# Scores by queries and again by keys in the first attention of a two-layer gated kernel

## The chip, the cores and the metric

The kernel runs on one core of a Trainium2 chip. A core has five engines that work side by side: TensorE (PE, with its weight loads listed as PEld), VectorE (DVE), ScalarE (ACT), GpSimd (POOL) and SyncE (SP), which here issues most DMAs. Each runs its own instructions in order and waits for the others by semaphores. The metric is the device time of one execution in microseconds (us), the median of several runs. Lower is better.

## The reference

The input is 16 sequences of 112 tokens of width 256, and for each sequence a context of 375 rows of width 256. Two layers follow one another, each a gated cross-attention and a gated feed-forward with experts. Everything is in 32-bit floats. The change touches only the first attention, which has 16 heads of width 16:

```
xn = layernorm(x)                                  # 16 x 112 x 256
q, k, v = xn@Wq + bq,  ctx@Wk + bk,  ctx@Wv + bv   # per head, 16 wide
w = softmax(q @ k.T / 4)                           # 112 x 375 for each head
x = x + tanh(g_xattn[0]) * ((w @ v).joined @ Wo + bo)
x = x + tanh(g_ffn[0]) * experts0(layernorm(x))    # 14 routed (best 2), 2 shared
x = x + tanh(g_xattn[1]) * attention1(layernorm(x), ctx)
x = x + tanh(g_ffn[1]) * experts1(layernorm(x))
```

The layer norm in front of the first attention has no weights.

## The kernel before

The tokens lie 128 to a tile, 14 tiles (NT). The first attention works on one sequence b at a time, and within it on four quads c of four heads each. That gives 64 quads, and the main loop of the first attention has one step n for each. A head is 16 wide and its slot in the array is 32 rows (HP), so four heads fill the 128 rows. The rows of a slot hold two heads of k; q has zeros in the half of the slot that the quad does not use.

A step before the change has these pieces, in the order in which they are written:

- `scores` (lines 506 to 525) makes q·k for quad n: 4 products with 32 rows each, one for each row group of the array, queries (112) on the partitions of the result and keys (375) along it. VectorE takes the maximum of each row, negated (line 520), and ScalarE makes the exponentials with that maximum as bias (line 522), into `p`.
- `apply` (line 539) multiplies the turned exponentials of quad n - 2 by the values, 12 products (3 chunks of 125 keys, 4 heads), each in one column group of the array. The values carry a column of ones, so the sums of the softmax come with them.
- `turn` (line 527) turns `p` of quad n - 1, so that keys lie on the partitions: 12 transposes on TensorE, and 4 copies out of PSUM, two on VectorE (line 535) and two on ScalarE (line 537).
- Side work, put by hand at a step and at one of three places in it by `at(step, place, f, ...)` and run by `beside`: keys (line 432), values (443) and queries (460) of a coming sequence, the two transposes that bring the result of a sequence into rows of channels (`first_turn`, `second_turn`), the output projection (`project`), the layer norm of the feed-forward behind it (`measured1`, `normed1`, `turned1`) and the logits of its router.

All of this is under `tc.manual_schedule()`: each engine runs its instructions in the order in which they are written. Constants and gates ahead of it (lines 109 to 161) are placed by the planner. In PSUM, `scores` has two slots of two banks, `bank()` three single banks in turn, and the result of `apply` one.

Each product of 32-bit floats is recorded as two weight loads and two matmuls, and each transpose as one of each. So `scores` shows 8 matmuls a step, `apply` 24, `turn` 12.

Ahead of step 0 the program measures and turns the first four token tiles, makes the keys, queries and values of sequence 0 and the scores of quad 0, and turns tiles 4 and 5. After the last quad, eight pieces of the shared experts (`hidden_piece`, `output_piece`) run one to a step, until the logits of the last token tile are made. The shared experts then go on, with the routing beside them, and the routed experts follow.

Of the kernel before, what the change touches and what calls it, by code (L numbers as in the profile page):

```python
# [51 lines left out]
def tile_flamingo(  # L52
# [55 lines left out]

    ident = const.tile([P, P], F32, tag="ident", name="ident")
    make_identity(nc, ident)  # L110

    bits_i = const.tile([P, 1], I32, tag="bits_i", name="bits_i")
    nc.gpsimd.iota(bits_i, pattern=[[0, 1]], base=0, channel_multiplier=1)
    nc.vector.tensor_scalar(bits_i, bits_i, HD, None, ALU.bitwise_and)
    halves = const.tile([P, 2], F32, tag="halves", name="halves")
    nc.vector.tensor_copy(halves[:, 1:2], bits_i)
# [38 lines left out]
    nc.scalar.activation(tg, rows_sb[:, 4 * D : 4 * D + 4], AF.Tanh)  # L155

    rowsg = const.tile([P, 4, D], F32, tag="rowsg", name="rowsg")
    for j, g in enumerate((0, 1, 3, 3)):
        nc.vector.tensor_scalar(
            rowsg[:, j, :], rows_sb[:, j * D : (j + 1) * D], tg[:, g : g + 1], None, ALU.mult  # L160
        )
# [252 lines left out]

    with tc.tile_pool(name="a0", bufs=2) as a0, tc.tile_pool(
        name="a0_s", bufs=2, space=PSUM
    ) as ps_s, tc.tile_pool(name="a0_t", bufs=3, space=PSUM) as ps_t, tc.tile_pool(
        name="a0_o", bufs=1, space=PSUM
    ) as ps_o, tc.manual_schedule():
# [5 lines left out]
        bqs = a0.tile([P, NQ], F32, tag="bqs", name="bqs", bufs=1)  # L425
        G = 4
        kts, qts, xns = {}, {}, {}

        def bank():
            return ps_t.tile([P, 512], F32, tag="t", name="pt")  # L430

        def keys(b, c):
            if c == 0:
                kts[b] = a0.tile([P, KD, S], F32, tag="kt", name="kt")
            pk = bank()[:, :S]
            for k in range(KD):
                nc.tensor.matmul(  # L437
                    pk, wk0_sb[:, k, c * P : (c + 1) * P], ctxs[b][:, k, :],
                    start=(k == 0), stop=(k == KD - 1),
                )  # L440
            nc.vector.tensor_scalar(kts[b][:, c, :], pk, col("bk0", c), None, ALU.add)

        def values(b, s0, n):
            pv = bank()[:SC].rearrange("p (j d) -> p j d", d=D)
            for j in range(n):
                s = s0 + j
                for k in range(KD):
                    nc.tensor.matmul(  # L448
                        pv[:, j, :], ctxs[b][:, k, s * SC : (s + 1) * SC], wv0_sb[:, k, :],
                        start=(k == 0), stop=(k == KD - 1),  # L450
                    )
            for j in range(n):
                to = vas[b % 2][:, s0 + j, :, 0:HD]
                v = pv[:, j, :].rearrange("p (h k) -> p h k", k=HD)
                if n == 1:
                    nc.scalar.copy(to, v)
                else:
                    nc.vector.tensor_copy(to, v)

        def queries(b0, g):  # L460

            if g == 0:
                qts[b0 // G] = a0.tile([P, NQ, G * TQ], F32, tag="qt", name="qt")
            pq = bank()[:, : G * TQ]
            for k in range(KD):
                nc.tensor.matmul(
                    pq, wq0_sb[:, k, g * P : (g + 1) * P],
                    xT[:, k, b0 * TQ : (b0 + G) * TQ],
                    start=(k == 0), stop=(k == KD - 1),
                )  # L470
            for u in range(2):
                c = 2 * g + u
                nc.scalar.activation(  # L473
                    qts[b0 // G][:, c, :], pq, AF.Identity, bias=bqs[:, c : c + 1],
                    scale=halves[:, u : u + 1],
                )
# [29 lines left out]
        def scores(b, c):  # L506
            qt, kt = qts[b // G], kts[b]
            t0 = (b % G) * TQ
            sps = [ps_s.tile([P, 2, 512], F32, tag="s", name="sp") for _ in range(2)]
            for j in range(4):  # L510
# [3 lines left out]
                    qt[r : r + HP, c, t0 : t0 + TQ], kt[r : r + HP, c // 2, :],  # L514
                    start=True, stop=True,
                )
            p = a0.tile([TQ, 4, S], F32, tag="p", name="p")
            for h, sp in enumerate(sps):
                mx = a0.tile([TQ, 2], F32, tag="mx", name="mx", bufs=4)
                nc.vector.tensor_reduce(mx, sp[:TQ, :, :S], AX.X, ALU.max, negate=True)  # L520
                for j in range(2):
                    nc.scalar.activation(  # L522
                        p[:, 2 * h + j, :], sp[:TQ, j, :S], AF.Exp, bias=mx[:, j : j + 1]
                    )
            return p

        def turn(p, pT, j):
            pp = bank()[:SC, : NSC * TQ]
            for s in range(NSC):
                nc.tensor.transpose(  # L530
                    pp[:, s * TQ : (s + 1) * TQ], p[:, j, s * SC : (s + 1) * SC],
                    ident[:TQ, :TQ],
                )
            if j % 2 == 0:
                nc.vector.tensor_copy(pT[:, j, :], pp)  # L535
            else:
                nc.scalar.copy(pT[:, j, :], pp)  # L537

        def apply(b, c, pT, po):
            va = vas[b % 2]  # L540
            for s in range(NSC):
                for j in range(4):
                    r = j * HP
                    nc.tensor.matmul(  # L544
                        po[r : r + HP, c, :], va[:, s, (c // 2) * 8 + j * 2 + c % 2, :],
# [3 lines left out]

        outs = {}  # L550
# [13 lines left out]
        def second_turn(b):  # L564
# [4 lines left out]
            for k in range(KD):  # L569
                nc.vector.tensor_scalar(  # L570
                    oT[:, k, b * TQ : (b + 1) * TQ], pt[:, k, :], col("bv0", k), None, ALU.add
                )
# [31 lines left out]
        def turned1(i):  # L604
# [6 lines left out]
            nc.vector.tensor_copy(xT[:, :, i * P : (i + 1) * P], pt)  # L611
# [14 lines left out]
        def at(step, place, f, *args):  # L626
            side.setdefault((step, place), []).append((f, args))


        hT = hidden_rows()  # L630

        def score_bank():
            return ps_s.tile([P, 2, 512], F32, tag="s", name="pd")[:, 0, :]

        pieces = [(hidden_piece, (score_bank, hT, 0, *blocks[0], m)) for m in range(KH)]
        pieces += [
            (output_piece, (score_bank, hT, 0, blocks[0][0], j)) for j in range(blocks[0][1])
        ]
        for n, (f, args) in enumerate(pieces):
            at(last + n, 0, f, *args)  # L640

        at(8, 2, shared_weights, 0)
        at(10, 2, shared_weights, 1)
        for i in (0, 2, 4):
            at(4 + i // 2, 2, biased, i)

        for i, n in ((6, 1), (8, 5), (10, 0), (12, 4)):
            at(n, 2, measured, i)
            at(n + 2, 2, normed0, i)
            at(n + 3, 1, turned, i)  # L650
            at(n + 3, 2, biased, i)
        for b in range(B):
            n0 = b * NQ
            if b + 2 < B:
                at(n0, 0, context, b + 2)
            if b + 1 < B:
                at(n0, 0, keys, b + 1, 0)
                at(n0 + 1, 0, keys, b + 1, 1)
                at(n0 + 1, 1, values, b + 1, 2, 1)
                at(n0 + 2, 0, values, b + 1, 0, 2)  # L660
# [3 lines left out]
            at(n0 + NQ + 2, 1, first_turn, b)  # L664
            at(n0 + NQ + 3, 0, second_turn, b)
        for i in range(NT):
            n = (((i + 1) * P - 1) // TQ + 2) * NQ
# [4 lines left out]
            at(n + 5, 1, logits, i)  # L672


        nc.vector.tensor_scalar(bqs, col("bq0", 0, NQ), HD**-0.5, None, ALU.mult)
        measured(0)
        measured(2)
        for t in vas:
            nc.gpsimd.memset(t, 0.0)
            nc.gpsimd.memset(t[:, :, :, HD : HD + 1], 1.0)  # L680
        normed0(0)
        turned(0)
        normed0(2)
        turned(2)
        keys(0, 0)
        queries(0, 0)
        ps, pTs = {0: scores(*quads[0])}, {}
        keys(0, 1)
        queries(0, 1)
        values(0, 0, 2)  # L690
        values(0, 2, 1)
        measured(4)
        normed0(4)
        turned(4)
        po = None

        def beside(n, place):
            for f, args in side.get((n, place), ()):
                f(*args)

        for n in range(max(side)[0] + 1):
            if 0 < n < last:
                ps[n] = scores(*quads[n])
            ended = None
            if 0 <= n - 2 < last:
                b, c = quads[n - 2]
                if c == 0:
                    po = ps_o.tile([P, NQ, TQ], F32, tag="av", name="po")
                apply(b, c, pTs.pop(n - 2), po)
                ended = b if c == NQ - 1 else None  # L710
            beside(n, 0)
            turning = 0 <= n - 1 < last
            if turning:
                pTs[n - 1] = a0.tile([SC, 4, NSC * TQ], F32, tag="pT", name="pT")
                for j in range(2):
                    turn(ps[n - 1], pTs[n - 1], j)
            if ended is not None:
                outs[ended] = a0.tile([P, NQ, TQ], F32, tag="oS", name="oS")
                nc.scalar.copy(outs[ended], po)
            beside(n, 1)  # L720
            if turning:
                for j in range(2, 4):
                    turn(ps[n - 1], pTs[n - 1], j)
                ps.pop(n - 1)
            beside(n, 2)

# [534 lines left out]
```

## Time and profile before

| what | before |
|---|---|
| median of 4 runs | 1044.06 us (1041.44 to 1046.28) |
| the profiled execution's own time | 1039.07 us |
| its span, first to last instruction | 1037.4 us |
| mean granted TensorE clock | 0.981 |
| PE busy in the span | 959.6 us (93%), 6474 matmuls |
| DVE busy | 552.5 us (53%) |
| ACT busy | 355.6 us (34%) |
| POOL busy | 184.3 us (18%) |
| 0 to 32.94 us (up to the scores of quad 1) | PE busy 17.5 us, granted clock 0.95 |
| 32.94 to 377.68 us (scores of quad 1 to those of quad 63) | PE 320.3, DVE 237.9, ACT 196.7, POOL 54.7 us busy, clock 1.00 |
| 377.68 to 405.37 us (up to the rest of the shared experts) | PE 25.6 us busy |
| 405.37 to 456.7 us (shared experts, routing) | PE 49.9 us busy |

In the profile, a line "out<-in" names the tile that an instruction writes and those that it reads. The count after "x" is the number of instructions; "busy" is their union, so overlapping ones count once. The idle time of a group is what its engine waited just before it, with the releaser. A matmul's own duration runs from its issue to its modelled end, and several are in flight, so the distance between starts tells more than the duration. In the timeline, each line gives the start and the length of a run of like instructions.

### The profile page before, as it was taken

How to read it: one execution, taken by the hardware profiler on the slowest of the kernel's cores; microseconds unless marked ns; L12 is line 12 of the kernel's file. 1: busy time of each engine (PE TensorE's matmuls, PEld its weight loads, DVE VectorE, ACT ScalarE, POOL GpSimd, SP SyncE). 2: the span in 40 equal slices, each digit the busy share in tenths (PEclk: the TensorE clock that was granted, in tenths of full speed). 3: DMA queues.
4: the chain of work that ended last, by engine and by line, in shares of the span. 5: the costliest groups of instructions: out<-in, count | busy, mean ns of one | idle time of the engine just before them, and what ended most of it. 6: DMA issues, size and time to landing. Idle time of an engine off the chain costs nothing.

```text
span 1037.4 us, 16798 instructions
## 1 busy us (share of the span) xinstructions
PE 959.6 (93%) x6474; PEld 711.1 (69%) x6474; DVE 552.5 (53%) x1352; ACT 355.6 (34%) x757; POOL 184.3 (18%) x323
## 2 busy tenths in 40 slices
PE   5899999999999989999999997899998999999995
PEld 2566666666666656688888883767786676666664
DVE  4676667676667754722222224364444756565675
ACT  2456555555655553101111111114222322222232
POOL 2251111111111112032222206350005000000033
PEclk9999999999999999999999999889998999999998
DMA  6400001001002000429999963234420000000001
GB/s 233 153 2 1 21 21 41 21 21 36 1 21 66 27 6 11 163 72 329 330 319 313 322 230 94 75 120 139 144 75 1 1 21 21 1 1 1 1 30 41
DMA packets 34303, 91.43 MB, mean 88 GB/s; under 512 B 4288, under 2 KB 17984, under 8 KB 28976
## 3 DMA queue, kind: packets, MB, share of 16 engines
q1 hardware_dynamic: 30368, 80.79, 23.1%
q0 software_dynamic: 3312, 9.05, 3.2%
q8 instruction: 51, 0.84, 0.3%
q10 hardware_dynamic: 544, 0.52, 0.1%
q14 instruction: 28, 0.23, 0.1%
HBM read 81.31 MB, written 9.04 MB: 87 GB/s over the span
## 4 chain that ended last, share of the span: by engine, by line
PE 73%; DVE 9%; DMA 7%; ACT 4%; issue 2%; another core or an unknown queue 2%; POOL 0%; SPq 0%; POOLq 0%; DVEq 0%; ACTq 0%
PE ph L1088 9%; PE py L1118 9%; DMA wr_sb<-in_wr_dram 7%; PE sp L512 5%; PE pt L448 5%; PE pt L437 5%; PE phr L763 4%; PE pt L530 4%; PE pyr L775 4%; PE po L544 3%; PE py L403 3%; PE po L998 2%; ACT p L522 2%; PE ph L393 2%
## 5 line engine op out<-in xcount | busy, mean ns | idle before, releaser
L522 ACT ACTIVATE p<-sp,mx 112x375 f32<-112x375 f32 x256 | 125.7, 574 | 96.1 <-DVE mx L520 96.1
L520 DVE TENSOR_REDUCE mx<-sp 112x2 f32<-112x750 f32 x128 | 114.1, 933 | 35.5 <-PE sp L512 32.8
L530 PE MATMUL pt<-ident,p 112*125 112x112 f32 x768 | 110.9, 276 | 16.8 <-DVE oT L570 10.4
L530 PEld LDWEIGHTS pt<-ident,p 112*125 112x125 f32 x768 | 100.4, 188 | 36.1 <-DVE oT L570 12.5
L1088 PE MATMUL ph<-w1b_sb,xT 128*128 128x512 f32 x224 | 102.1, 600 | 0.0
L1118 PE MATMUL py<-w2b_sb,hT 128*128 128x256 f32 x448 | 100.8, 382 | 0.0
L1118 PEld LDWEIGHTS py<-w2b_sb,hT 128*128 128x128 f32 x448 | 82.2, 190 | 14.0 <-ACT hT L1110 4.2
L763 PE MATMUL phr<-xgT,wr_sb 128*128 128x128 f32 x656 | 83.8, 281 | 5.4 <-DVE xgT L753 5.0
L535 DVE COPY pT<-pt 125x336 f32<-125x336 f32 x128 | 64.1, 501 | 42.3 <-PE pt L530 42.2
L763 PEld LDWEIGHTS phr<-xgT,wr_sb 128*128 128x128 f32 x656 | 77.5, 191 | 11.4 <-DVE xgT L753 11.2
L753 DVE TENSOR_SCALAR xgT<-px,wr_sb 128x128 f32<-128x128 f32 x82 | 25.0, 347 | 113.0 <-DMA wr_sb<-in_wr_dram 97.7
L174 POOL TENSOR_SCALAR rstd<-mv 128x1 f32<-128x1 f32 (+2 forms) x23 | 5.2, 224 | 420.2 <-DVE mv L167 420.2
L775 PE MATMUL pyr<-wr_sb,hTr 128*128 128x256 f32 x328 | 77.4, 379 | 0.0
L768 ACT ACTIVATE hTr<-phr 128x512 f32<-128x512 f32 x41 | 24.5, 597 | 152.2 <-PE phr L763 136.1
L537 ACT COPY pT<-pt 125x336 f32<-125x336 f32 x128 | 56.6, 442 | 49.5 <-PE pt L530 48.4
L1088 PEld LDWEIGHTS ph<-w1b_sb,xT 128*128 128x128 f32 x224 | 41.7, 191 | 42.4 <-issue 38.7
L744 POOL DMA_INDIRECT xg_sb<-xn_rows,taker x41 | 39.0, 952 | 155.0 <-PE px L751 115.6
L775 PEld LDWEIGHTS pyr<-wr_sb,hTr 128*128 128x128 f32 x328 | 59.3, 190 | 6.4
L1095 ACT ACTIVATE rh<-mvh,eps 128x1 f32<-128x1 f32 x56 | 16.3, 292 | 131.4 <-DVE mvh L167 131.4
L544 PEld LDWEIGHTS po<-pT,va 125*32 125x32 f32 x1536 | 35.7, 109 | 36.0 <-issue 31.0
L512 PE MATMUL sp<-kt,qt 32*112 32x375 f32 x512 | 57.6, 519 | 0.8 <-ACT qt L473 0.8
L544 PE MATMUL po<-pT,va 125*32 125x112 f32 x1536 | 52.8, 263 | 0.4 <-ACT pT L537 0.4
(231 smaller groups left out, 1466.3 us busy)
## 6 DMA issues: line engine op xcount, KB each, us to landing
wr_sb<-in_wr_dram SPq DMA_DIRECT2D x41, 1025.0 KB
ctx_sb<-in_ctxT_dram SPq DMA_DIRECT2D x32, 375.0 KB
ctxn_sb<-in_ctxN_dram SPq DMA_DIRECT2D x16, 375.0 KB
yg<-yr SPq DMA_DIRECT2D x41, 128.0 KB
w1b_sb<-in_w1b_dram SPq DMA_DIRECT2D x4, 512.0 KB
w2b_sb<-in_w2b_dram SPq DMA_DIRECT2D x4, 512.0 KB
xn_rows<-xn SPq DMA_DIRECT2D x14, 128.0 KB
out_dram<-yf SPq DMA_DIRECT2D x14, 128.0 KB
```

The costliest lines, as they stand in the source:

```text
L437: nc.tensor.matmul(pk, wk0_sb[:, k, c * P : (c + 1) * P], ctxs[b][:, k, :], start=(k == 0), stop=(k == KD - 1),)
L512: nc.tensor.matmul(sps[j // 2][:TQ, j % 2, :S], qt[r : r + HP, c, t0 : t0 + TQ], kt[r : r + HP, c // 2, :], start=True, stop=True,)
L520: nc.vector.tensor_reduce(mx, sp[:TQ, :, :S], AX.X, ALU.max, negate=True)
L522: nc.scalar.activation(p[:, 2 * h + j, :], sp[:TQ, j, :S], AF.Exp, bias=mx[:, j : j + 1])
L530: nc.tensor.transpose(pp[:, s * TQ : (s + 1) * TQ], p[:, j, s * SC : (s + 1) * SC], ident[:TQ, :TQ],)
L535: nc.vector.tensor_copy(pT[:, j, :], pp)
L537: nc.scalar.copy(pT[:, j, :], pp)
L544: nc.tensor.matmul(po[r : r + HP, c, :], va[:, s, (c // 2) * 8 + j * 2 + c % 2, :], pT[:, j, s * TQ : (s + 1) * TQ], start=(s == 0), stop= ...
L763: nc.tensor.matmul(ph[:, m, :], a[:, k, m * P : (m + 1) * P], xgT[:, k, :], start=(k == 0), stop=(k == KD - 1),)
L775: nc.tensor.matmul(py, hT[:, m, :], c[:, m, :], start=(m == 0), stop=(m == KH - 1))
L1088: nc.tensor.matmul(ph, xT[:, k, i * P : (i + 1) * P], a[:, k, :], start=(k == 0), stop=(k == KD - 1),)
L1118: nc.tensor.matmul(py, hT[:, m, j * P : (j + 1) * P], c[:, m, :], start=(m == 0), stop=(m == KH - 1),)
```

## The change

`scores` makes only the maxima. The exponentials are taken from a second product, made by keys. For this, each half of a slot gets its own copy of the keys: in copy u one row of the slot that q leaves at zero is set to one. The negated maximum of each query is put in that same row of q, so the product by keys comes out with the maximum already taken off, and ScalarE makes the exponential without a bias, in the layout that `apply` needs. `turn` is gone. `scores` needs the matching copy of the keys too, and there the row of q is still zero.

The order of a step is now: `scores(n)`, `apply(n - 2)`, side place 0, `maxima(n)`, side place 1, `turned_scores(n)`, side place 2. In PSUM there are two named pairs of banks, for scores and for the side work of places 1 and 2, and four named single banks, for the product by keys, for `apply`, for the turned maxima and for the side work of place 0. Every one has one buffer.

```
+    written = ExitStack()
+    written.enter_context(tc.manual_schedule())      # now from the constants on
...
+    # spots[:,0:2]: one in row 16 (0) of each slot; spots[:,2:4] = 1 - spots[:,0:2]
+    def gated(j):                                     # was at the start
+        if j == 0:
+            nc.scalar.activation(tg, rows_sb[:, 4 * D : 4 * D + 4], AF.Tanh)
+        g = (0, 1, 3, 3)[j]
         nc.vector.tensor_scalar(
             rowsg[:, j, :], rows_sb[:, j * D : (j + 1) * D], tg[:, g : g + 1], None, ALU.mult
         )
...
+        def pair(h):
+            return ps_s.tile([P, 2, 512], F32, tag=f"s{h}", name=f"sp{h}")
+        def single(j):
+            return ps_t.tile([P, 512], F32, tag=f"t{j}", name=f"pt{j}")
         def bank():
+            n, place["n"] = place["n"], place["n"] + 1
+            if place["at"] == 0:
+                return single(1 + n % 2)
+            if n % 2 == 0:
+                place["pair"] = pair(n // 2 % 2)
+            return place["pair"][:, n % 2, :]
...
         def keys(b, c):
-            nc.vector.tensor_scalar(kts[b][:, c, :], pk, col("bk0", c), None, ALU.add)
+            nc.vector.tensor_scalar(
+                kts[b][:, c, 0, :], pk, spots[:, 2:3], bks[:, c, 0:1], ALU.mult, ALU.add
+            )
+            nc.scalar.activation(
+                kts[b][:, c, 1, :], pk, AF.Identity, bias=bks[:, c, 1:2], scale=spots[:, 3:4]
+            )
-        def values(b, s0, n):        # two chunks (DVE copies) or one (ACT copy)
+        def values(b, s):            # one chunk, copied by ACT
...
         def queries(b0, g):          # two outputs: were both ACT, now one DVE, one ACT
...
         def scores(n):
             ...                      # the 4 products as before, on kt[..., u, :]
-            p = a0.tile([TQ, 4, S], F32, tag="p", name="p")
             for h, sp in enumerate(sps):
-                mx = a0.tile([TQ, 2], F32, tag="mx", name="mx", bufs=4)
-                nc.vector.tensor_reduce(mx, sp[:TQ, :, :S], AX.X, ALU.max, negate=True)
-                for j in range(2):
-                    nc.scalar.activation(
-                        p[:, 2 * h + j, :], sp[:TQ, j, :S], AF.Exp, bias=mx[:, j : j + 1]
-                    )
+                nc.vector.tensor_reduce(
+                    mz[:, 2 * h : 2 * h + 2, HD * (1 - u)], sp[:TQ, :, :S], AX.X, ALU.max,
+                    negate=True,
+                )
-        def turn(p, pT, j):          # 3 transposes and a copy; 4 calls a step
+        def maxima(n):
+            pm = single(3)[:, :TQ]
+            nc.tensor.transpose(pm, mzs[c % 2], ident[:TQ, :TQ])
+            qms[n] = a0.tile([P, TQ], F32, tag="qm", name="qm")
+            nc.vector.tensor_tensor(qms[n], pm, qts[b // G][:, c, t0 : t0 + TQ], ALU.add)
+        def turned_scores(n):
+            sts = [single(j) for j in range(4)]
             for s in range(NSC):
                 for j in range(4):
                     r = j * HP
+                    nc.tensor.matmul(
+                        sts[j][:SC, s * TQ : (s + 1) * TQ],
+                        kt[r : r + HP, c // 2, c % 2, s * SC : (s + 1) * SC], qm[r : r + HP, :],
+                        start=True, stop=True,
+                    )
+            pT = a0.tile([SC, 4, NSC * TQ], F32, tag="pT", name="pT")
+            for j in range(4):
+                nc.scalar.activation(pT[:, j, :], sts[j][:SC, : NSC * TQ], AF.Exp)
+            return pT
         def apply(n, pT):            # into single(0), copied by ACT every step
...          # second_turn's result and turned1's: DVE -> ACT
-            at(last + n, 0, f, *args)                 # the eight expert pieces
+            at(last + n, 1, f, *args)
+        for j in range(4):
+            at(1 + j // 2, 2, gated, j)
-        for i, n in ((6, 1), (8, 5), (10, 0), (12, 4)):
+        for i, n in ((4, 3), (6, 7), (8, 15), (10, 19), (12, 23)):
             at(n, 2, measured, i); at(n + 2, 2, normed0, i); at(n + 3, 0, turned, i)
+        at(0, 0, values, 0, 0)
+        at(0, 1, queries, 0, 1)
         for b in range(B):
             n0 = b * NQ
+            at(n0, 0, values, b, 1);  at(n0, 1, keys, b, 1);  at(n0 + 1, 0, values, b, 2)
             if b + 1 < B:
+                at(n0 + 2, 1, keys, b + 1, 0);  at(n0 + 3, 0, values, b + 1, 0)
-            at(n0 + NQ + 2, 1, first_turn, b);  at(n0 + NQ + 3, 0, second_turn, b)
+            at(n0 + NQ + 1, 1, first_turn, b);  at(n0 + NQ + 2, 0, second_turn, b)
         for i in range(NT):
-            n = (((i + 1) * P - 1) // TQ + 2) * NQ
+            b = ((i + 1) * P - 1) // TQ + 1
+            n = b * NQ + 3 if b % G < G - 2 else (b + 1) * NQ + 1
             at(n, 1, project, i);  at(n, 2, measured1, i)
             at(n + 2, 2, normed1, i);  at(n + 3, 0, turned1, i)
-            at(n + 5, 1, logits, i)
+            at(n + 4, 0, logits, i)
+        # ahead of step 0: POOL's memsets of va (and of the two mz) first, then
+        # measured(0), measured(2), normed0(0), normed0(2), keys(0, 0), turned(0),
+        # turned(2), queries(0, 0); the rest of sequence 0 is in steps 0 and 1
```

## The prediction

> **What bounds the kernel now.** The page first: busy times and the costliest groups.
>
> ```profile
> PE 959.6 (93%) x6474; PEld 711.1 (69%) x6474; DVE 552.5 (53%) x1352; ACT 355.6 (34%) x757; POOL 184.3 (18%) x323
> ...
> L520 DVE TENSOR_REDUCE mx<-sp 112x2 f32<-112x750 f32 x128 | 114.1, 933 | 35.5 <-PE sp L512 32.8
> L530 PE MATMUL pt<-ident,p 112*125 112x112 f32 x768 | 110.9, 276 | 16.8 <-DVE oT L570 10.4
> ```
>
> PE sets the time; the transposes of line 530 are its costliest group. Second, the windows by stage: quads 1 to 63, the tail to 405.37, shared experts to 456.7, routed experts.
>
> ```profile
> 32.94:377.68 344.74, 320.27 (x3243) 229.04 (x3243) 237.89 (x449) 196.67 (x428) 54.70 (x134) 1.00 0.09 28
> 377.68:405.37 27.69, 25.56 (x183) 18.02 (x183) 10.76 (x27) 8.70 (x17) 5.79 (x18) 1.00 0.05 15
> 405.37:456.70 51.33, 49.88 (x213) 34.99 (x213) 29.36 (x105) 10.26 (x16) 4.45 (x5) 1.00 0.26 93
> 456.70:661.00 204.30, 188.03 (x1144) 161.49 (x1145) 52.06 (x158) 30.37 (x53) 57.44 (x61) 0.97 0.77 256
> ```
>
> PE is 93% busy in the loop, 97% in the shared experts behind it; DMA fills the routed experts, which start when PE ends the shared ones. So what the first attention saves moves all that follows. 62 steps take 344.74 us: 5.56 each. Third, the timeline of one step (200.63 to 206.63).
>
> ```profile
> 200.63 0.29 PEld L512 LDWEIGHTS sp<-kt,qt 32*112 32x112 f32 x8
> 200.63 0.90 PE L512 MATMUL sp<-kt,qt 32*112 32x375 f32 x8
> ...
> 201.46 0.78 PE L544 MATMUL po<-pT,va 125*32 125x112 f32 x24
> ...
> 201.63 1.78 DVE L520 TENSOR_REDUCE mx<-sp 112x2 f32<-112x750 f32 x2
> ...
> 202.17 0.41 PE L568 MATMUL pt<-ident,o 112*128 112x112 f32 x2
> ...
> 204.37 1.69 PE L466 MATMUL pt<-xT,wq 128*128 128x448 f32 x4
> ...
> 205.89 0.81 PE L530 MATMUL pt<-ident,p 112*125 112x112 f32 x6
> ```
>
> Starts give PE's prices: scores 0.83 (200.63 to 201.46), apply 0.71 (to 202.17), queries 1.52 (204.37 to 205.89), six transposes 0.74 (205.89 to the next scores at 206.63). Distances between starts elsewhere in the timeline give keys 1.37, one chunk of values 0.91, a projection 0.97, `first_turn` 0.45. Fourth, the timeline of the start.
>
> ```profile
> 9.64 3.82 DVE L486 TENSOR_SCALAR xnp<-x_sb,mv,rstd 128x256 f32<-128x256 f32 x4
> ...
> 29.56 1.09 PE L501 MATMUL pt<-ident,xnp 128*128 128x128 f32 x4 [2.78 <-DVE xnp L486]
> ...
> 32.94 0.29 PEld L512 LDWEIGHTS sp<-kt,qt 32*112 32x112 f32 x8 [0.91 <-issue]
> ```
>
> Scores of quad 1 start only at 32.94: PE waited 2.78 us for tiles 4 and 5, and the four norms took 0.95 us each beside POOL's memsets of `va` (10.08 to 13.26; a norm of line 599 takes 0.41).
>
> **The change, part by part.** *PE work.* Out go 12 transposes: 2 x 0.74 = 1.48 us a step. In come one transpose (0.11, the pitch in a run of them) and 24 matmuls by keys. No row shows those; their nearest are line 544 (24 matmuls, 112 columns moving, four at once, 0.71) and line 512 (32 rows, four row groups). I take 0.75, near line 544. At least it is six passes of four at 0.096, 0.58; if all 24 ran singly at the transposes' 0.11 pitch, it is 2.6. So PE's work shrinks by about 1.48 - 0.11 - 0.75 = 0.62 us a step; what the time makes of it hangs on the waits.
>
> *The new wait.* `maxima` needs both reduces of its own quad; before, transposes of the previous quad stood there. From the start of scores: 1.00 to the first reduce (200.63 to 201.63), 1.78 for both, 0.05 to PE: the transpose starts at 2.83. Queued behind it on PE are places 1 and 2, the product by keys and the next scores. Covering it are scores 0.83, apply 0.71 and place 0: values leave it covered to 2.45, with logits or a tile's transposes to 2.8. PE idles 0.03 (2.83 - 2.8) to 1.3 us (empty place 0). Then the transpose 0.36 (361 ns in line 530's longest), 0.04, the addition 0.28 (half of line 570's pair, 0.57), 0.05: the product can start at 3.56, and place 1 runs meanwhile. The next scores follow 0.75 later, if place 1's PSUM pair is read out by then.
>
> - Free place 1: 3.56 + 0.75 = 4.31 (`first_turn` fits in).
> - Keys (1.37): 2.83 + 0.11 + 1.37 + 0.10 to change shape + 0.75 = 5.16. The copies (608 ns, side by side on DVE and ACT) end at 5.09, inside.
> - `first_turn` and projection: 2.83 + 0.11 + 0.45 + 0.97 + 0.10 + 0.75 = 5.21; projection alone 4.76.
> - Queries: the 0.72 us copy ends last, 5.45.
>
> The schedule puts keys in 30 of steps 1 to 62, queries in 6, `first_turn` with a projection in 7, a projection alone in 5; 14 are free. Sum: 30 x 5.16 + 6 x 5.45 + 7 x 5.21 + 5 x 4.76 + 14 x 4.31 = 308 us against 344.7: **-36.6**.
>
> *Copies and exponentials.* DVE loses two copies of 0.50 (line 535) a step and gains 0.28; ACT trades 4 exponentials and 2 copies (1.96 + 0.88) for 4 exponentials over 336 columns (1.8 to 1.96), a small copy, and its share of keys, values and `second_turn`, some 3.2 us of a step of 5. Neither binds. Exponentials of step n - 1 end some 2.3 us into step n, before `maxima` needs the last single bank at 2.83; if they ended later, PE would wait for ACT instead. `apply` needs the first bank at 0.83 and gets it at about 0.85. These moves I cost at nothing; uncovered, they cost what passes 2.83.
>
> *Start.* POOL's memsets now come before its powers and so run while the tokens load (no cover is needed before 8 us); the norms take 1.6 instead of 3.8. Keys of sequence 0 move ahead of the turned tiles; the two query copies run side by side, saving 0.6. Scores of quad 0 come at about 16.3 instead of 20.33. Step 0 then takes 2.83 + 0.11 + 1.52 + 1.37 + 0.10 + 0.75 = 6.7, and the wait for tiles 4 and 5 is gone: quad 1 at 23 to 24.5 instead of 32.94. The early clock may stay low (0.95 here), so I take **-8.5**, of 6 to 10.
>
> *Once-only costs.* `gated` moves to steps 1 and 2. Its Tanh queues behind that step's exponentials on ACT, and two DVE products of 0.34 wait for it ahead of the next step's reduces: +2.1. In two steps place 0 holds three items for two banks: +1. **+3.** `normed1`'s DMA on SP moves with its step and lands long before the routing; the contexts stay at their steps.
>
> *Tail.* From the scores of quad 63: 4.3, two applies, eight pieces of 1.9, two projections, two turned tiles, two logits, `first_turn` and `second_turn`: 26 against 27.7. **-2.** Logits now come before the last piece, not after, so the routing waits no longer than before.
>
> Sum: -36.6 - 8.5 + 3 - 2 = -44. The profiled execution took 1039.07 (span 1037.4 and 1.7 around it) and becomes 995; the median of the runs is 5.0 above the profiled one, so **1000**.
>
> **Two rules of the Trainium skill.** Row: eight loads of line 512 (170 ns each) end 0.29 us after the first, while its first four matmuls run to about 201.03 in the same row groups; so loads hide, and 0.75 stands. Against the change speaks "TensorE: Matmul & The Clock Gate", Part 3, "The mechanism": a load overlaps running matmuls only when the row group differs. By that rule the sum would lose the whole gain, as the slower rival below. Row: from the last transpose to the next scores is 0.20 instead of 0.11. "TensorEngine Tiling (Array Packing)", "Key Properties", says that a change of tiling mode drains the array. The step has three such changes before and after, since the product by keys and the next scores share a shape; by the rule as by the row nothing is added.
>
> **The rivals.**
>
> 1. *Loads that do not hide (slower).* If each of the six groups of four paid its load and its pass in turn, 0.17 + 0.096 (apply's pitch per four, 0.71 less 0.13 over six), the product by keys takes 1.60, 0.85 more on PE in each of 64 steps: +54, so 1054. It decides from a product of 0.75 + 44/64 = 1.44 us. For it: no 32x125 load is in the trace. Against it: line 512 above.
> 2. *A longer chain.* Each hand-over costs 0.1 more, or the exponentials hold the last bank past 2.83: 0.35 a step, +22: 1022. For it: every link is now serial, with single buffers. Against it: each link's row is above.
> 3. *PE alone binds.* If side work fills all waits, PE's work per sequence is 4 x (0.83 + 0.71 + 0.11 + 0.85) + 2.7 values + 2.7 keys + 0.8 queries + 2.1 for the rest = 18.3, 4.6 a step: 62 x 0.37 = 23 less than the sum above: 977 to 980.
> 4. *The change gives nothing.* Waits take back all of the 0.6 us a step: about 1044, less or more by the start.
>
> **How the numbers follow.** The likeliest, 985 to 1012 around 1000: 0.50. Rival 2 (1012 to 1036): 0.26. Rival 3 (975 to 985): 0.12. Rival 1: 0.08. Rival 4: 0.04. The range 980 to 1034 leaves out the slower ones and some of the ends: about 0.2. A difference of 0.5%, 5.2 us, is about what a measurement of this kernel tells from none: faster 0.88, same 0.04, slower 0.08.
>
> **What would show it.** Scores at 4.3 to 5.5 us from each other, mean near 5.0; quad 1's scores near 23.5. The product by keys 0.7 to 0.8 from its start to the next scores. PE idle before the transpose of `mz`, released by DVE; ACT and DVE below 75% there. The forecast is wrong if the product by keys takes over 1.4, if PE waits for an ACT copy or exponentials rather than for the reduces, or if the steps with free place 1 take over 5.

## The result

The changed kernel takes 1047.05 us in the median of 52 runs, against 1044.05 us for the kernel before (78 runs). The ratio is 1.0027, with a 95% interval of 1.0013 to 1.0040. The forecast of 1000 us was wrong: nothing was gained.

The profiled execution took 1044.11 us, its span is 1042.4 us. First the page after, with busy times and two groups of the first attention; `scores` is now line 544, its reduce line 551, the product by keys line 572.

```profile
PE 934.1 (90%) x7306; PEld 665.7 (64%) x7306; DVE 499.6 (48%) x1225; ACT 317.8 (30%) x779; POOL 185.7 (18%) x325
...
L551 DVE TENSOR_REDUCE mz<-sp 112x2 f32<-112x750 f32 x128 | 114.2, 935 | 75.2 <-PE sp L544 74.8
...
L544 PE MATMUL sp<-kt,qt 32*112 32x375 f32 x512 | 56.1, 506 | 26.3 <-ACT kt L476 19.9
```

The group of `scores` before the change:

```profile
L512 PE MATMUL sp<-kt,qt 32*112 32x375 f32 x512 | 57.6, 519 | 0.8 <-ACT qt L473 0.8
```

Every engine but POOL does less work than before: PE lost 25 us of busy time, DVE 53, ACT 38. Yet the time did not fall. `scores`, for which PE had waited 0.8 us in the whole run, now waits 26.3 us, most of it for ScalarE's copy of the keys. The windows of the changed kernel, from the scores of quad 1 to those of quad 63, and from there to the first routed product, say where:

```profile
27.50:374.67 347.17, 293.74 (x4062) 184.70 (x4066) 187.69 (x333) 160.07 (x449) 56.54 (x136) 1.00 0.11 33
...
374.67:457.11 82.44, 74.72 (x401) 50.86 (x396) 37.00 (x122) 19.81 (x39) 10.20 (x23) 0.98 0.18 63
```

The 62 steps take 347.2 us, 2.4 more than before, where 308 had been forecast; PE is busy in 85% of them, against 93%. The start is 5.4 us shorter (quad 1's scores at 27.50 instead of 32.94). The way from quad 63 to the first routed product takes 82.4 us instead of 79.0. In sum the routed experts start at 457.1 instead of 456.7. What the profile shows beyond that, 4.6 us of the 5.0, lies behind 457 us: near 790 us this one execution ran 20.5 us at half clock, that of the kernel before 6.8. The medians differ by 3.0; what they consist of behind 457 us, one profile of each kernel does not tell.

The timeline of a step with keys (its scores start at 203.63, the next at 209.52) shows the new wait. The bracket at the end of a line says how long the engine was idle and what released it.

```profile
207.99 0.92 PE L572 MATMUL pt<-qm,kt 32*125 32x112 f32 x24
208.10 0.67 DVE L473 TENSOR_SCALAR kt<-sp,spots,bks 128x375 f32<-128x375 f32 x1 [1.01 <-PE sp L469]
208.80 0.66 ACT L476 ACTIVATE kt<-sp,bks,spots 128x375 f32<-128x375 f32 x1 [1.82 <-DVE kt L473]
...
209.52 0.90 PE L544 MATMUL sp<-kt,qt 32*112 32x375 f32 x8 [0.61 <-ACT kt L476]
```

The product of the keys is done at about 208.1. VectorE makes its copy to 208.77. ScalarE, which has nothing else to do, starts 0.03 us later and ends at 209.46. Only then is the PSUM pair free, and the scores of the next quad start at 209.52. The two copies go one after the other. The releaser is read from semaphores, so it is the program as built that holds ScalarE back. Over the loop, the list of waits has this line for each of the 30 steps with keys, as total, count and longest, and one for the scores that wait in turn:

```profile
ACT kt L476 <- DVE kt L473: 69.0, 30, 4.7
...
PE sp L544 <- ACT kt L476: 19.2, 30, 0.7
```

In the 7 steps with `first_turn` and a projection, there is another wait: PE holds the projection back until VectorE has read the turned sums, which lie in the other bank of the same PSUM tile.

```profile
368.63 1.13 PE L625 MATMUL sp<-wo,oT 128*128 128x256 f32 x4 [0.81 <-DVE o L609]
```

### The profile page after: what moved, and what is told of

It reads as the page before. It is cut to its first block, busy times and chain, and to the rows that moved or that the text cites. A ratio compares the mean times of both kernels' runs of the same rounds, so it can differ in the third digit from the quotient of the medians.

```text
span 1042.4 us, 18262 instructions
## 1 busy us (share of the span) xinstructions
PE 934.1 (90%) x7306; PEld 665.7 (64%) x7306; DVE 499.6 (48%) x1225; ACT 317.8 (30%) x779; POOL 185.7 (18%) x325
## 4 chain that ended last, share of the span: by engine, by line
PE 70%; DVE 12%; DMA 7%; ACT 5%; issue 3%; another core or an unknown queue 2%; POOL 1%; DVEq 0%; POOLq 0%; ACTq 0%
PE ph L1125 10%; PE py L1155 9%; DMA wr_sb<-in_wr_dram 7%; DVE mz L551 6%; PE sp L544 5%; PE phr L800 4%; PE sp L469 4%; PE pyr L812 4%; PE ph L406 4%; PE py L416 3%; PE po L1035 2%; PE pt L572 2%; DVE kt L473 2%; ACT kt L476 2%
## 5 line engine op out<-in xcount | busy, mean ns | idle before, releaser
L551 DVE TENSOR_REDUCE mz<-sp 112x2 f32<-112x750 f32 x128 | 114.2, 935 | 75.2 <-PE sp L544 74.8
L579 ACT ACTIVATE pT<-pt 125x336 f32<-125x336 f32 x256 | 94.1, 456 | 54.2 <-PE pt L572 54.2
L1125 PE MATMUL ph<-w1b_sb,xT 128*128 128x512 f32 x224 | 105.3, 615 | 0.0
L544 PE MATMUL sp<-kt,qt 32*112 32x375 f32 x512 | 56.1, 506 | 26.3 <-ACT kt L476 19.9
L572 PEld LDWEIGHTS pt<-qm,kt 32*125 32x125 f32 x1536 | 47.8, 183 | 29.9 <-issue 25.5
L572 PE MATMUL pt<-qm,kt 32*125 32x112 f32 x1536 | 59.0, 282 | 3.1 <-DVE qm L563 3.1
L591 PEld LDWEIGHTS pt<-pT,va 125*32 125x32 f32 x1536 | 35.0, 110 | 35.4 <-ACT pT L579 34.6
L483 PE MATMUL pt<-wv,ctx_sb 128*125 128x256 f32 x192 | 53.9, 404 | 0.0
L591 PE MATMUL pt<-pT,va 125*32 125x112 f32 x1536 | 50.6, 265 | 0.6 <-ACT pT L579 0.6
L416 PE MATMUL py<-w_sb,hT 128*128 128x256 f32 x192 | 44.3, 390 | 7.5 <-DVE mv L180 7.5
```

The costliest lines, as they stand in the source:

```text
L416: nc.tensor.matmul(py, hT[:, m, j * P : (j + 1) * P], c[:, m, :], start=(m == 0), stop=(m == KH - 1),)
L483: nc.tensor.matmul(pv, ctxs[b][:, k, s * SC : (s + 1) * SC], wv0_sb[:, k, :], start=(k == 0), stop=(k == KD - 1),)
L544: nc.tensor.matmul(sps[j // 2][:TQ, j % 2, :S], qt[r : r + HP, c, t0 : t0 + TQ], kt[r : r + HP, g, u, :], start=True, stop=True,)
L551: nc.vector.tensor_reduce(mz[:, 2 * h : 2 * h + 2, HD * (1 - u)], sp[:TQ, :, :S], AX.X, ALU.max, negate=True,)
L572: nc.tensor.matmul(sts[j][:SC, s * TQ : (s + 1) * TQ], kt[r : r + HP, c // 2, c % 2, s * SC : (s + 1) * SC], qm[r : r + HP, :], start=True ...
L579: nc.scalar.activation(pT[:, j, :], sts[j][:SC, : NSC * TQ], AF.Exp)
```

## The experiments

Theory A: the copies are serial because both engines read one PSUM bank, and the rest of the prediction's sum is right. Theory B: they are serial because both write one tile in SBUF. Theory C: the serial chain from scores over the maxima to the product by keys sets every step, and the copies only lie beside it.

**1. A tile for each copy of the keys.** The edit:

```
-                kts[b] = a0.tile([P, KD, 2, S], F32, tag="kt", name="kt")
+                kts[b] = [a0.tile([P, KD, S], F32, tag=f"kt{u}", name=f"kt{u}") for u in range(2)]
```

> The two copies of the keys go to two tiles of their own in SBUF; nothing else differs from the changed kernel. Theory A (the second copy waits because it reads the same PSUM bank as the first): ACT still starts when DVE ends, 0.67 us later; steps with keys stay at 5.8 to 6.0 us, the time at 1042 to 1050. Theory B (it waits because both write one tile): the copies run side by side, those steps fall to about 5.2, and the time falls by 30 x 0.7 = 21 us, to about 1024.

The one run took 1046.94 us, steps with keys 5.8 to 6.0 us in 25 of the 30. The timeline of such a step:

```profile
210.63 0.67 DVE L473 TENSOR_SCALAR kt<-sp,spots,bks 128x375 f32<-128x375 f32 x1 [1.00 <-PE sp L469]
...
211.33 0.67 ACT L476 ACTIVATE kt<-sp,bks,spots 128x375 f32<-128x375 f32 x1 [1.82 <-DVE kt L473]
```

ScalarE still starts 0.03 us after VectorE ends (210.63 + 0.67 = 211.30). Theory B falls: it is not the common tile of the results that makes ScalarE wait.

**2. Two banks for each product of keys and of queries.** Half of the columns go to a bank of each pair; ScalarE makes both copies of the first half, VectorE both of the second:

```
+            for h, (s0, s1) in enumerate(((0, 188), (188, S))):
+                pk = half(h)[:, : s1 - s0]               # pair(h)[:, 0, :] in place 1
                 ...                                       # the product, columns s0 to s1
+                for u in range(2):
+                    (ACT if h == 0, DVE if h == 1): kts[b][:, c, u, s0:s1] <- pk
```

> Each product of keys and of queries goes to two banks of two PSUM tiles, half of the columns in each; ACT makes both copies of one half, DVE both of the other. Copies of 375 and 448 columns become pairs of 188 and 224 on each engine. Theory A: the copies end 0.7 us earlier, steps with keys fall from 5.8 to 6.0 to about 5.2, with queries from 6.27 to about 5.5: 30 x 0.7 + 6 x 0.8 = 26 us, 2 more at the start; about 1019 against 1047, 0.975 of the kernel before. Theory C (the chain from scores over maxima to the product by keys sets every step, and the copies lie beside it): steps with keys stay over 5.7, and the time over 1037.

Measured: 1016.09 us, ratio to the kernel before 0.973 (0.967 to 0.979). Steps with keys fell from 6.02 to 5.28 us, those with queries from 6.27 to 5.37. The timeline of a step with keys (its scores start at 185.57, the next at 190.85):

```profile
189.58 0.91 ACT L480 ACTIVATE kt<-sp,bks,spots 128x188 f32<-128x188 f32 x2 [0.33 <-PE sp L473]
...
190.22 0.85 DVE L485 TENSOR_SCALAR kt<-sp,spots,bks 128x187 f32<-128x187 f32 x2 [1.01 <-PE sp L473]
...
190.85 1.16 PE L563 MATMUL sp<-kt,qt 32*112 32x375 f32 x8
```

Each engine is now released by PE alone, and their copies overlap (190.22 to 190.49). There are more instructions than before the edit and no less work, yet 31 us are gone. Theory C falls with it: the chain over the maxima is as long as it was (free steps take 4.47 us, against 4.41). Both engines still read the same constants (`spots`, `bks`), so these are not what made ScalarE wait. What is left is the place in PSUM that both read. The edit gave each engine its own bank and also its own PSUM tile; no run separates the two, so whether the wait goes by the bank or by the tile stays open.

**3. Two products of place 1 in two tiles.** The edit:

```
-            if n % 2 == 0:
-                place["pair"] = pair(n // 2 % 2)
-            return place["pair"][:, n % 2, :]
+            return pair(n % 2)[:, 0, :]
```

> Two products in place 1 of one step get banks of two PSUM tiles, not two banks of one tile. If the projection waits for the reads of the turned sums only because they share a tile, the 7 steps with both fall from 6.21 to about 5.2 us, step 0 from 9.3 to about 7.8, and the tail loses two or three waits of 0.7: about 10 us, 1037 against 1047. If the projection needs those reads for another reason: no change, 1047.

Measured: 1034.31 us, ratio 0.9917 (0.9877 to 0.9957). That is 0.8% under the kernel before, and the interval lies clear of that of the changed kernel (1.0013 to 1.0040). The 7 steps fell from 6.21 to 5.14 us, 7.5 in all. The group of the projections in the loop, first in the changed kernel, then here, shows no idle time ahead of it any more:

```profile
L625 PE MATMUL sp<-wo,oT 128*128 128x256 f32 x48 | 13.1, 396 | 5.7 <-DVE o L609 5.7
...
L623 PE MATMUL sp<-wo,oT 128*128 128x256 f32 x48 | 12.4, 381 | 0.0
```

So the wait came from the common tile, not from the data. Step 0 did not fall (9.3 us). The wait of its keys for the copies of the queries is gone there too, 1.60 us in the changed kernel. But in this execution its scores and values took 5.1 us up to the turned maxima (18.16 to 23.27), against 2.9 in the changed kernel (18.16 to 21.03). A low clock at the start would fit that, but the granted clock is recorded only from 24.2 us on. The way from quad 63 to the first routed product lost 0.7 us, not two or three waits.

**4. All of it.** Experiments 2 and 3 together, and the gates ahead of step 0:

```
-        for j in range(4):
-            at(1 + j // 2, 2, gated, j)
...
         queries(0, 0)
+        for j in range(4):
+            gated(j)
```

> The split copies, the banks apart, and the gates (Tanh and its four products) made ahead of step 0 instead of in steps 1 and 2. Theory A, with all else of the sum of the prediction right: 26 + 2 + 10 + 2 = 40 us, about 1007 against 1047, 0.965 of the kernel before; steps with keys near 5.2, free ones near 4.3, mean near 5.0. Theory C: over 1030.

Measured: 1003.95 us, ratio 0.9596 (0.9528 to 0.9663). The windows of the loop and of the way to the first routed product:

```profile
23.36:334.27 310.91, 292.61 (x4214) 212.85 (x4211) 193.34 (x366) 172.96 (x484) 56.33 (x136) 1.00 0.12 37
334.27:417.28 83.01, 76.14 (x402) 51.72 (x397) 37.00 (x122) 19.80 (x39) 10.17 (x23) 0.96 0.17 63
```

PE is busy in 94% of the loop, and the loop takes 310.9 us. The forecast's sum was 308. By kind of step, in us, from the distances between the starts of the scores in one profiled execution of each:

| steps 1 to 62 | count | forecast | changed | 2: split | 3: apart | 4: all |
|---|---|---|---|---|---|---|
| keys in place 1 | 30 | 5.16 | 6.02 | 5.28 | 6.01 | 5.19 |
| queries | 6 | 5.45 | 6.27 | 5.37 | 6.27 | 5.37 |
| `first_turn` and projection | 7 | 5.21 | 6.21 | 6.27 | 5.14 | 5.20 |
| projection alone | 5 | 4.76 | 4.71 | 4.79 | 4.71 | 4.79 |
| free | 14 | 4.31 | 4.41 | 4.47 | 4.41 | 4.47 |
| sum | 62 | 308 | 347.2 | 321.2 | 339.3 | 310.9 |

Experiments 2 and 3 move their own rows and leave the others within 0.08 us. Step 2, which is among those with keys, takes 7.37 us in the changed kernel, 8.02 in experiment 2 and 5.09 here, where neither the gates nor a second copy hold it up.

**5. Both copies on one engine.** The keys by VectorE alone, the queries by ScalarE alone:

```
-            nc.scalar.activation(
-                kts[b][:, c, 1, :], pk, AF.Identity, bias=bks[:, c, 1:2], scale=spots[:, 3:4]
-            )
+            nc.vector.tensor_scalar(
+                kts[b][:, c, 1, :], pk, spots[:, 3:4], bks[:, c, 1:2], ALU.mult, ALU.add
+            )
```

> The changed kernel, but both copies of the keys are made by DVE and both of the queries by ACT; nothing else differs. Theory A (two engines that read one bank go one after the other): two copies on one engine take as long as two on two engines, so steps with keys stay at 5.8 to 6.0 us, those with queries near 6.2, and the time at 1043 to 1051. If the division over two engines was worth something in spite of the wait, steps with keys take 6.3 or more and the time rises by over 10 us.

Measured: 1043.61 us, ratio 1.0019 (0.9993 to 1.0046). Steps with keys take 5.91 us instead of 6.02, those with queries 6.11 instead of 6.27. A step with keys:

```profile
208.52 0.67 DVE L473 TENSOR_SCALAR kt<-sp,spots,bks 128x375 f32<-128x375 f32 x1 [1.00 <-PE sp L469]
...
209.10 0.66 DVE L476 TENSOR_SCALAR kt<-sp,spots,bks 128x375 f32<-128x375 f32 x1
```

The second copy starts 0.58 us after the first, without a handover; on two engines it was 0.70 (208.10 to 208.80 in the changed kernel). So the division over two engines was worth nothing, and in the loop a little less than nothing.

**6. The banks behind the last quad.** Experiment 4, and from step 64 on the expert pieces take the two pairs in turn and all else in place 1 a single bank:

```
+            if place["step"] >= B * NQ:
+                return single(3)
             return pair(n % 2)[:, 0, :]
+        def piece_bank(m):
+            return lambda: pair(m % 2)[:, 0, :]
```

> All three edits of the fourth experiment, and after the last quad the expert pieces take the two pairs in turn and everything else in place 1 a single bank. From the scores of quad 63 to the first routed product the fourth experiment took 83.0 us against 79.0 before the change, where the prediction had a gain of 2. If waits of 0.7 for ScalarE's read of the one pair cause it: 2 to 4 us less, near 1000. If the chain over the layer norm of the last tokens and the lower clock after the wait for the last maxima cause it: no change, 1004.

Measured: 1002.80 us, ratio 0.9611 (0.9576 to 0.9647), which the runs can't tell from experiment 4. In the windows, the way from quad 63 to the first routed product is shorter:

```profile
334.32:414.10 79.78, 73.75 (x402) 51.11 (x397) 36.99 (x122) 19.81 (x39) 10.17 (x23) 0.98 0.18 65
```

79.8 us instead of 83.0. But the clock in it was higher too (0.98 against 0.96: 3.4 us at half clock instead of 6.8, some 1.7 us of PE time), so that of the 3.2 us no more than about half can be put down to the banks; one execution of each is not enough to say more.

## Why the prediction was wrong

**The step that failed** is the one sentence on place 1 with keys: "The copies (608 ns, side by side on DVE and ACT) end at 5.09, inside", and its like for queries. They ran one after the other, and took 0.67 and 0.66 us, against 0.61 for the one copy before (line 441):

```profile
210.07 0.61 DVE L441 TENSOR_SCALAR kt<-pt,cols 128x375 f32<-128x375 f32 x1 [0.66 <-PE pt L437]
```

The second one ends 0.7 us later, past the product by keys that was to cover it. The steps with keys and with queries took (6.02 - 5.16) x 30 + (6.27 - 5.45) x 6 = 31 us more than their terms. Of this, 3 us are the once-only costs below, for which the prediction had a term of its own; so some 28 us are the copies. The row that I took for them, line 441, had one copy for each bank. In the loop before, VectorE and ScalarE both read a bank of scores only where the second needs the first's result (the maximum), so "side by side" had no row behind it, and I gave it no price from the other side.

A page of the Trainium skill bears on this: "PSUM — Partial Sum Buffer", section "PSUM bank collisions raise a hardware error", says that two different engines on one bank and the same 32 partitions collide, reads against reads included, and asks for a semaphore between them. The trace shows the wait, 30 times of 30, ScalarE starting 0.03 to 0.04 us after VectorE ends; the collision itself no run here shows. Whether the copies could overlap on one bank without the wait was not tried.

**A second step failed the same way:** "`first_turn` and projection: 5.21". The two share a PSUM tile, though not a bank, and the program makes PE wait for the reads of the first before it writes the second: (6.21 - 5.21) x 7 = 7 us. The loop missed its sum by 39 us (347.2 against 308): some 28 are the copies, 7 the common tile, 3 the once-only costs, and about 1 the free steps at 4.41 instead of 4.31. With both steps mended, and the gates moved, it took 310.9.

**What was right.** The price of PE's work: the product by keys takes 0.71 us from its start to the next scores (357.69 to 358.40 in the changed kernel) where I took 0.75.

```profile
357.69 0.92 PE L572 MATMUL pt<-qm,kt 32*125 32x112 f32 x24 [0.46 <-DVE qm L563]
...
358.40 0.84 PE L544 MATMUL sp<-kt,qt 32*112 32x375 f32 x8
```

The loads of 32 by 125 hide, as line 512 had promised. (The prediction's 201.03 is the start of the second four matmuls there; the first four are recorded to end at 201.19 to 201.21. The loads end at 200.91, so the reading holds.) The slower rival by loads was wrong. The time came nearest to rival 4 (about 1044, chance 0.04), which says that waits take the gain back but not which; the mechanism itself was not among the rivals. The chain over the maxima: 4.41 us for a free step against 4.31. Rival 2, a longer chain of 0.35 a step, is not what happened, for the free steps would show it. Once-only costs: step 2, which waits for the gates, took 1.4 us more than the plain steps with keys (7.37 against 5.92), where 2.1 had been forecast. Steps 22 and 26, with three items in place 0, took 0.3 more each, where 1 in all had been forecast. Steps 20 and 24 took 0.7 and 0.4 more, which had not: VectorE's statistics for a layer norm stand ahead of the reduces there, and the first reduce starts 1.70 and 1.38 us after the scores instead of about 0.9. The sum, 3.1 for a term of 3, is right partly by luck.

**What was off in size.** The start gained 5.4 us, not 8.5: the copies of keys and queries there are serial too, and PE waits 1.60 and 0.68 us for the second of them in step 0 (and 1.60 ahead of the scores of quad 0). With split copies it gained 9.8 (experiment 2) and 9.6 (experiment 4). The clock of the start has a part in such numbers: experiment 1, whose start has the same copies, had 10.2 us at half clock there and gained 3.6. The way behind the last quad lost 3.4 us, where 2 of gain were forecast: pieces in one pair wait 0.69 us for ScalarE's read, the last turned tiles wait 1.0 each for their norm, and PE ran at half clock for 3.4 us shortly after quad 63 began.

**The range** ended at 1034 because no bound in it let the copies of the keys run one after the other. Of the other copies and exponentials the prediction says "These moves I cost at nothing; uncovered, they cost what passes 2.83"; for these there was no such price. Steps with keys were the most frequent kind, and their cover ended only 0.07 us after the copies (5.16 against 5.09). A second copy behind the first would have made it 5.09 + 0.67 = 5.76, and 30 times 0.60 is 18 us that the range should have held as a bound. Of the signs that I named for a wrong forecast, it was the wait "for an ACT copy or exponentials rather than for the reduces" that came.

## What to carry to other kernels

Here two engines that copied from one PSUM bank worked one after the other, and dividing the copies over VectorE and ScalarE gained nothing until each had a bank, and a tile, of its own: half of the columns to each turned 1047 us into 1016. Two products in flight together did better in two PSUM tiles than in two banks of one (5.14 us a step against 6.21). When a term of a sum rests on "side by side", look for a row in which these two engines do just that on the same data, and price the other case if there is none.

## What was not expected of the hardware

Twenty-four loads and matmuls of 32 rows by 125 columns, in four row groups, take 0.71 us, although each load alone is recorded with 184 ns: six rounds of four start 0.11 us from each other, the second one 0.20 after the first. And at the end of the loop, where free steps leave PE waiting (1.25 us ahead of the last maxima), the granted clock fell to half for 3.4 to 6.8 us near the scores of quad 63 in the profiled execution of the changed kernel and of all six experiments; in the one of the kernel before it did not. Whether the waits cause this, no run separates.
